# A graph attention layer: identity and root table first, sources turned in four pieces, half of the normalising on VectorE, small sums on POOL

## The chip, the cores and the metric

The kernel runs on one core of a Trainium2 chip. The core has five engines, each with its own in-order queue: TensorE (PE in the profile; PEld are its weight loads), VectorE (DVE), ScalarE (ACT), GpSimd (POOL) and SyncE (SP), which here only issues transfers. The engines wait for each other through semaphores alone. The metric is the device time of one execution in microseconds; the median of several runs counts.

## What is computed

Each of 12,500 nodes has a row x of 128 numbers; 212,500 edges, sorted by their target node, have attributes, a weight, a source and a target. The reference, cut to what matters:

```python
h = jnp.maximum(_layernorm(x, axis=-1), 0.0)
q = (h @ Wq.T + bq).reshape(N, NUM_HEADS, HEAD_DIM)          # 8 heads of 16
k = (edge_h @ Wk.T + bk).reshape(-1, NUM_HEADS, HEAD_DIM)
v = (h @ Wv.T + bv).reshape(N, NUM_HEADS, HEAD_DIM)
qs, qd = (q[src], q[dst])
in_m, out_m, diag_m = (qs * k).sum(-1), (qd * k).sum(-1), (qs * qd).sum(-1)
att = jnp.power(distance, lam)
score = (softmax(in_m * SCALE, dst) + softmax(out_m * SCALE, dst) + softmax(diag_m * SCALE, dst)) * att
agg = segment_sum(score[..., None] * v[dst], dst)
out = x + leaky_relu(agg.reshape(N, 128) @ Wo.T + bo, 0.1)
```

The three softmaxes run over the edges of one target node. The change touches only the first two lines and the preparation beside them: layer norm, ReLU, and the product with Wq.

## The kernel before

`ordered_path` does all the work for sorted targets. It has two parts.

**The preparation** (lines 690 to 982) fills two tables in DRAM: `q_table`, with one row of q for each node in float32, and `q3_table`, with the same row as three bfloat16 terms. The nodes lie in 98 tiles of 128 rows in one SBUF buffer `xq`, loaded in nine pieces by transfers on SP's queue. Four tiles make a group; there are 24 groups of four and one of two. The loop at line 925 runs over the groups g as a software pipeline. One turn of it issues, in this order:

- `rectify(g + 2)`, line 860: normalises and rectifies four tiles in place on ScalarE, one instruction for each tile, as ReLU(x * inv + shift), with inv and shift one number a row.
- `turn_h(g + 1)`, line 865: four transposes on TensorE through the identity matrix `ident` into one PSUM tile, then one ScalarE copy of 512 columns to `hT`.
- `nodes_q(g)`, line 873: four products with Wq into PSUM, one VectorE addition of the bias (line 880) back into `xq`, and the store of the group's rows to `q_table` on SP's queue (line 881).
- `ready(g + 4)` and `measure(...)`: the statistics, a few groups ahead. `statistics` (line 829) takes a loaded piece of 4, 4, 6 or 14 tiles: one bn_stats for each tile on VectorE, then five small VectorE operations on as many columns as there are tiles (lines 839 to 844), the "small sums". `scale` (line 847) makes inv and shift of them: a square root on ScalarE, a reciprocal and one more operation on VectorE.
- one entry of `side` (line 907), at the turns named there. `edges_0` lets POOL cast the source and target indices to float; `turn_ws` turns three weights; `biases` splits the biases in terms; `edges_1` turns the sources; `edges_2` turns the edge weights; `edges_3` makes thresholds and relative targets.

`turn_edges` (line 758) works on a quarter of the edges at a time: four transposes on TensorE into a PSUM tile `t_ps`, and one VectorE copy out of it (line 764). The pool of `t_ps` has two buffers, so the third quarter waits for the copy of the first. `edges_1` takes all four quarters at once. After it `step` may be written (line 782, POOL), since it lies where the sources lay.

After the loop POOL issues the first gathers (`gather`, line 645): indirect transfers of 128 rows of `q_table` each, which wait for all stores to that table. Then `terms_q` (line 887) makes and stores the three terms.

**The main loop** (line 1371) runs over 415 blocks of 512 edges. For each one POOL issues four gathers, twelve blocks ahead; TensorE turns and projects the edge attributes and spreads the targets' rows; VectorE multiplies and sums the logits; scans over the edges make the softmaxes' maxima.

What sets the order: `pin` (line 590) ties every instruction given to it behind the one pinned before it on the same engine. So the queues of the engines stand in the order in which the Python code runs. Instructions that aren't pinned, such as most constants at the top, are placed by the scheduler.

Of the kernel before, what the change touches and what calls it, by code (L numbers as in the profile page):

```python
# [7 lines left out]
F32 = mybir.dt.float32  # L8
BF = mybir.dt.bfloat16
I32 = mybir.dt.int32  # L10
AF = mybir.ActivationFunctionType
ALU = mybir.AluOpType
# [7 lines left out]
EPS = 1e-5  # L20
# [452 lines left out]
def ordered_path(ctx: ExitStack, tc: tile.TileContext, flag, x, src, dst, edge_attr, edge_weight,  # L473
# [19 lines left out]
    nc = tc.nc  # L493
    N, F = x.shape
    E = src.shape[0]
    P = 128
# [17 lines left out]
    NU, CU = NI // 2, 7  # L514
    CH = 2 * CU
# [6 lines left out]
    def parts_of(u):  # L522

        return [s for s in range(S)
                if (s == 0 or START * s - NEAR < UN * (u + 1))
                and (s == S - 1 or UN * u <= START * (s + 1) + NEAR)]
# [12 lines left out]
    sums = [dram.tile([NP, 2, 2 * H3], F32, name=f"sums{i}") for i in range(S)]  # L539


    consts = ctx.enter_context(tc.tile_pool(name="consts", bufs=1))
    jp = consts.tile([P, P], I32, name="jp")
    nc.gpsimd.iota(jp, pattern=[[1, P]], base=0, channel_multiplier=-1)
    ident = consts.tile([P, P], F32, name="ident")
    nc.vector.tensor_scalar(ident, jp, 0.0, None, op0=ALU.is_equal)

    third = consts.tile([P, 1], F32, name="third")
    threes = consts.tile([P, W], F32, name="threes")
    nc.gpsimd.iota(threes, pattern=[[3, W]], base=0, channel_multiplier=-1,  # L550
# [5 lines left out]
    ones3 = consts.tile([3, P], BF, name="ones3")  # L556
    nc.vector.memset(ones3, 1.0)

    eps = consts.tile([P, 1], F32, name="eps")
    nc.vector.memset(eps, EPS)  # L560
    wq, wv, wk, wo = [consts.tile([P, F], F32, name=n) for n in ("wq", "wv", "wk", "wo")]
    b3 = consts.tile([3, 3, F], BF, name="b3")
    bv3, bk3, bo3 = [b3[:, i, None, :].to_broadcast([3, JN, F]) for i in range(3)]
# [2 lines left out]
    inv = consts.tile([P, NI], F32, name="inv")  # L566
    shift = consts.tile([P, NI], F32, name="shift")
    blank = jp.bitcast(F32)[:, :2 * 2 * H3]
    nc.vector.memset(blank, 0.0)
    src_i = consts.tile([P, NB, JN], I32, name="src_i")  # L570
    att_t = consts.tile([P, NB, JN], F32, name="att_t")
# [12 lines left out]
    edges = ctx.enter_context(ExitStack())  # L584
    gath = edges.enter_context(tc.tile_pool(name="gath", bufs=QQ))
    load = edges.enter_context(tc.tile_pool(name="load", bufs=2))

    pinned = {}

    def pin(inst):  # L590

        engine = str(inst.ins.engine)
        if engine in pinned:
            tc.add_manual_dep(inst.ins, pinned[engine], mybir.DependencyInfo(
                mybir.DependencyClass.NoSync, mybir.DependencyReason.DATA), reason="in order")
        pinned[engine] = inst.ins.name
        return inst

    def rows_in(to, t, q):

        top, cut = (RW - 1) * RC, 96
        pin(q.dma_start(to[0:cut, :], t[:cut * RC].rearrange("(r c) -> r c", c=RC)))
        pin(q.dma_start(to[cut:RW - 1, :], t[cut * RC:top].rearrange("(r c) -> r c", c=RC)))
        pin(q.dma_start(to[RW - 1:RW, :E - top], t[None, top:E]))
# [85 lines left out]
    with tc.tile_pool(name="prep", bufs=1) as prep, \  # L690
# [10 lines left out]
        weight = prep.tile([RW, RC], F32, name="weight")  # L701
# [5 lines left out]
        xq = prep.tile([P, NI, F], F32, name="xq")  # L707
# [19 lines left out]
        for s in range(S):  # L727
            at = s * G * BE
            pin(nc.sync.dma_start(bases[:, :, s:s + 1], dst[None, at:at + G * BE + 1:BE, None]))
            n = min(T, (E - at - HEAD) // BE + 1)  # L730
            pin(nc.sync.dma_start(heads[:, :n, s:s + 1],
                                  dst[None, at + HEAD - 1:at + (n - 1) * BE + HEAD:BE, None]))
            n = min(T, (E - at) // BE)
# [24 lines left out]
        def turn_edges(of, to, which=range(RB)):  # L758
            cols = of.rearrange("r (a p j) -> r a j p", a=RB, j=JN)
            for a in which:  # L760
                t_ps = prep_ps.tile([P, JN, RW], F32, name="t_ps")
                for j in range(JN):
                    pin(nc.tensor.transpose(t_ps[:, j, :], cols[:, a, j, :], ident[:RW, :RW]))
                pin(nc.vector.tensor_copy(to[:, a:NB:RB, :], t_ps.rearrange("p j r -> p r j")))

        dst_f = dst_r.bitcast(F32)
        src_f = src_r.bitcast(F32)
# [6 lines left out]
        def edges_0():  # L774

            pin(nc.gpsimd.tensor_copy(src_f, src_r))
            pin(nc.gpsimd.tensor_copy(dst_f, dst_r))

        def edges_1():
            turn_edges(src_f, src_i)  # L780
            step = got["step"] = prep.tile([RW, RC + 1], F32, name="step", tag="step")
            pin(nc.gpsimd.tensor_sub(step, dst_f[:, 1:], dst_f[:, :RC + 1]))

        def edges_2():
            turn_edges(weight, att_t)

        def edges_3():
            of = got["cuts"] = of_tile()
# [20 lines left out]
        def turn_w(i, to):  # L809
            w_ps = prep_ps.tile([P, F], F32, name="t_ps")  # L810
            pin(nc.tensor.transpose(w_ps, w_in[:, i, :], ident))
            pin(nc.scalar.copy(to, w_ps))
# [16 lines left out]
        def statistics(lo, hi):  # L829

            n = hi - lo
            stats = node.tile([P, CH, 6], F32, name="stats", bufs=1)[:, :n]
            for i in range(n):
                pin(nc.vector.bn_stats(stats[:, i, :], xq[:, lo + i, :]))


            sums3 = node.tile([P, 3, CH], F32, name="sums3", bufs=4)[:, :, :n]
            total, apart, sq = sums3[:, 0], sums3[:, 1], sums3[:, 2]
            pin(nc.vector.tensor_add(total, stats[:, :, 1], stats[:, :, 4]))
            pin(nc.vector.tensor_sub(apart, stats[:, :, 1], stats[:, :, 4]))  # L840
            pin(nc.vector.tensor_add(sq, stats[:, :, 2], stats[:, :, 5]))
            pin(nc.vector.scalar_tensor_tensor(apart, apart, F / 4.0, apart, op0=ALU.mult,
                                               op1=ALU.mult))
            pin(nc.vector.tensor_add(sq, sq, apart))
            return lo, hi, total, sq

        def scale(lo, hi, total, sq):
# [9 lines left out]
        def tiles_of(g):  # L857
            return range(g * JN, min(NI, (g + 1) * JN))

        def rectify(g):  # L860
            for i in tiles_of(g):
                pin(nc.scalar.activation(xq[:, i, :], xq[:, i, :], AF.Relu, bias=shift[:, i:i + 1],
                                         scale=inv[:, i:i + 1]))

        def turn_h(g):
            n = len(tiles_of(g))
            h_ps = node_ps.tile([P, JN, P], F32, name="h_ps")
            for b, i in enumerate(tiles_of(g)):
                pin(nc.tensor.transpose(h_ps[:, b, :], xq[:, i, :], ident))
            hT = hTs[g] = node.tile([P, JN, P], F32, name="hT", bufs=2)  # L870
            pin(nc.scalar.copy(hT[:, :n], h_ps[:, :n]))

        def nodes_q(g):
            n = len(tiles_of(g))
# [12 lines left out]
        def terms_q(g):  # L887
# [8 lines left out]
            if g > 0:  # L896
# [7 lines left out]
                    q3_table[3 * lo:3 * (lo + n * P), :].rearrange("(u p k) f -> p u (k f)", p=P, k=6),  # L904
                    q3.rearrange("p (u k) t f -> p u (k t f)", k=2)))

        side = {0: edges_0, 4: turn_ws, 6: biases, 9: edges_1, 15: edges_2, 18: edges_3}
        turn_w(0, wq)
        parts = [(2 * lo, 2 * hi) for lo, hi in zip(LOADS, LOADS[1:])]

# [2 lines left out]
        def measure(upto):  # L913

            while parts and parts[0][0] < (upto + 1) * JN:
                measured.append(statistics(*parts.pop(0)))
# [8 lines left out]
        for g in range(-2, GN):  # L925
            if g + 2 < GN:
                rectify(g + 2)
            if 0 <= g + 1 < GN:
                turn_h(g + 1)
            if g >= 0:  # L930
                nodes_q(g)
            ready(g + 4)
            measure(g + 6 + min(max(g, 0), 6))
            if g in side:
                side[g]()
            if g == 9:
                fetch_edges(0)
                fetch_few()
# [161 lines left out]
    with tc.tile_pool(name="work", bufs=2) as work, \  # L1100
# [270 lines left out]
        for g in range(end):  # L1371
# [44 lines left out]
            if g < S:  # L1416
                of = [u for u in range(NU) if g in parts_of(u)]
# [56 lines left out]
@with_exitstack  # L1474
def kernel(ctx: ExitStack, tc: tile.TileContext, x, src, dst, edge_attr,
                              edge_weight, Wq, bq, Wk, bk, Wv, bv, Wo, bo, lam, out):

    nc = tc.nc  # L1480
    given = (x, src, dst, edge_attr, edge_weight, Wq, bq, Wk, bk, Wv, bv, Wo, bo, lam, out)
    flags = ctx.enter_context(tc.tile_pool(name="flags", bufs=1))
    flag = flags.tile([1, 1], I32, name="flag")
    ordered_path(tc, flag, *given)
    other = nc.values_load(flag[0:1, 0:1], min_val=0, max_val=1)
    with tc.If(other != 0):
        general_path(tc, *given)
# [29 lines left out]
```

## Time and profile before

| | |
|---|---|
| median of 7 runs | 2280.92 us (2274.59 to 2286.1) |
| the profiled execution, its own time | 2281.6 us |
| its span, first to last instruction | 2279.8 us |
| busy share of the span: PE, PEld, DVE, ACT, POOL | 74%, 59%, 87%, 59%, 73% |
| mean granted TensorE clock | 0.79 |
| first statistics on VectorE | at 4.33 us |
| first normalising on ScalarE | at 11.61 us |
| first store to q_table issued | at 50.64 us |
| last store to q_table issued | at 80.43 us |
| first gather | at 83.32 us |
| first block of the main loop on TensorE (L1133) | at 136.31 us |

The profile records one execution. Its rows name an instruction by its source line, its engine, and its output and inputs ("out<-in"). A number of instructions of one kind have a busy time, a mean duration and the idle time of the engine just before them, with what ended most of it. Two instructions of one engine can overlap by some 0.1 us, so start-to-start distances are used where a row of instructions is added up. All times are in microseconds from the start of the span, if nothing else is said.

### The profile page before, as it was taken

Reading aid. Unit: us, or ns where it says so; the run is one execution under the profiler, and the core shown is the slowest. Engines: PE = TensorE matmul, PEld = TensorE weight load, DVE = VectorE, ACT = ScalarE, POOL = GpSimd, SP = SyncE. Lnnn points to the kernel's source line nnn. Section 1 sums busy time; section 2 is a strip of 40 time slices with the busy share of each in tenths; the row PEclk is TensorE's granted clock in tenths of the full one; section 3 lists DMA queues with packets and bytes.
Section 4 is the critical chain, followed back from the end, with each engine's and each line's share of the span. In section 5 each row is a group of like instructions: output and inputs, shape, how many; then the busy total and the mean of one; then the engine's idle time right before and its main releaser. Section 6 shows DMA issues by size and latency. Waiting matters only on the chain.

```text
span 2279.8 us, 34664 instructions
## 1 busy us (share of the span) xinstructions
PE 1685.2 (74%) x10209; PEld 1341.1 (59%) x10209; DVE 1986.5 (87%) x2582; ACT 1346.3 (59%) x2445; POOL 1654.8 (73%) x1690
## 2 busy tenths in 40 slices
PE   5337887866767778877787778777786777777785
PEld 4335666655656556666565666656575666656564
DVE  7579999988989889898898998888898899889894
ACT  6646766655656556565565565555565565655571
POOL 3577777777777777777777777777777777777760
PEclk8768878877878887787778777777777887777777
DMA  6786455455445544455545554454545544555531
GB/s 196 246 269 184 146 162 168 139 158 150 138 146 149 164 141 141 145 167 149 147 141 168 152 147 137 144 171 141 148 132 163 161 143 140 145 166 150 151 100 56
DMA packets 314459, 351.19 MB, mean 154 GB/s; under 512 B 132882, under 2 KB 234013, under 8 KB 313952
## 3 DMA queue, kind: packets, MB, share of 16 engines
q1 hardware_dynamic: 245493, 233.57, 33.4%
q0 software_dynamic: 53344, 109.11, 17.3%
q10 hardware_dynamic: 15424, 6.19, 1.1%
q8 instruction: 83, 1.36, 0.2%
q14 instruction: 115, 0.94, 0.1%
HBM read 316.50 MB, written 32.17 MB: 153 GB/s over the span
## 4 chain that ended last, share of the span: by engine, by line
DMA 32%; PE 28%; DVE 18%; issue 12%; POOL 5%; ACT 5%; DVEq 0%; SPq 0%; ACTq 0%; POOLq 0%
DMA qq<-q_table,src_i 30%; PE k_ps L1125 10%; POOL qq L649 5%; PE w_ps L1272 5%; DVE prod L1145 4%; PE eT_ps L1116 4%; DVE prod L1146 3%; PE k_ps L1123 3%; DVE prod L1144 2%; PE qd_ps L1133 2%; PE node_ps L1056 2%; DMA q_table<-q 1%; DVE m L1212 1%; DVE back L1232 1%; PE d_ps L1258 1%
## 5 line engine op out<-in xcount | busy, mean ns | idle before, releaser
L649 POOL DMA_INDIRECT qq<-q_table,src_i x1660 | 1619.8, 976 | 512.8 <-issue 241.4
L1147 DVE TENSOR_REDUCE lT<-prod 128x96 f32<-128x1536 f32 x415 | 727.5, 1753 | 14.4
L1125 PEld LDWEIGHTS k_ps<-wk,eT 128*128 128x128 f32 x3320 | 514.6, 237 | 178.9 <-issue 69.3
L1125 PE MATMUL k_ps<-wk,eT 128*128 128x128 f32 x3320 | 608.7, 339 | 14.7 <-ACT eT L1118 14.3
L1133 PE MATMUL qd_ps<-win,oh 126*128 126x128 bf16 x1660 | 186.5, 244 | 422.6 <-DVE prod L1145 366.4
L1118 ACT COPY eT<-eT_ps 128x512 f32<-128x512 f32 x415 | 243.4, 587 | 356.9 <-PE eT_ps L1116 347.0
L1145 DVE TENSOR_TENSOR prod<-qq,qd_ps 128x512 f32<-128x512 f32 x415 | 283.2, 682 | 173.5 <-DMA qq<-q_table,src_i 172.3
L1133 PEld LDWEIGHTS <-oh 126*128 126x128 bf16 x1660 | 145.3, 109 | 483.1 <-issue 412.8
L1136 ACT COPY qd<-qd_ps 128x512 f32<-128x512 f32 x415 | 239.2, 576 | 144.7 <-PE qd_ps L1133 131.2
L1116 PE MATMUL eT_ps<-ident,ea 128*128 128x128 f32 x1660 | 316.8, 325 | 1.0 <-DVE found L954 1.0
L1110 ACT ACTIVATE relb<-relb,before 126x512 bf16<-126x512 bf16 x415 | 301.1, 726 | 0.0
L1144 DVE TENSOR_TENSOR prod<-qd,k_ps 128x512 f32<-128x512 f32 x415 | 279.3, 673 | 10.1 <-ACT qd L1136 5.7
L1146 DVE TENSOR_TENSOR prod<-qq,k_ps 128x512 f32<-128x512 f32 x415 | 282.6, 681 | 0.0
L1111 ACT ACTIVATE oh<-relb 126x512 bf16<-126x512 bf16 x415 | 261.4, 630 | 18.7 <-issue 5.5
L1116 PEld LDWEIGHTS eT_ps<-ident,ea 128*128 128x128 f32 x1660 | 253.8, 173 | 1.3 <-DVE found L954 1.3
L1272 PE MATMUL w_ps<-back,sel 128*126 128x144 f32 (+1 forms) x1344 | 209.7, 316 | 25.9 <-ACT sel L1262 21.1
L1272 PEld LDWEIGHTS w_ps<-back,sel 128*126 128x126 f32 (+1 forms) x1344 | 198.5, 215 | 35.4 <-ACT sel L1262 29.6
L1233 ACT ACTIVATE back<-back 128x480 f32<-128x480 f32 x83 | 50.1, 604 | 283.7 <-DVE back L1232 275.7
L1123 PE MATMUL k_ps<-b,ones 3*128 3x512 bf16 x415 | 184.3, 444 | 30.9 <-DVE prod L1146 28.9
L1200 DVE TENSOR_TENSOR_SCAN u<-far,u,l_ps 120x512 f32<-120x512 bf16 x82 | 104.4, 1273 | 9.6 <-PE l_ps L1167 6.9
L1212 DVE TENSOR_TENSOR_SCAN m<-far,head,u 120x512 f32<-120x512 bf16 x83 | 106.0, 1278 | 0.1
L1224 PE MATMUL m_ps<-ident,m 120*128 120x120 f32 x332 | 71.7, 355 | 40.2 <-DVE m L1212 39.1
(192 smaller groups left out, 1350.5 us busy)
## 6 DMA issues: line engine op xcount, KB each, us to landing
ea<-in_edge_attr_dram SPq DMA_DIRECT2D x83, 1280.0 KB
relb<-rel_d SPq DMA_DIRECT2D x83, 630.0 KB
qq<-q_table,src_i POOLq DMA_INDIRECT x1660
win<-q_table SPq DMA_DIRECT2D x415, 31.5 KB
far<-far_d SPq DMA_DIRECT2D x84, 120.2 KB
q_table<-q SPq DMA_DIRECT2D x24, 384.0 KB
sums<-rows SPq DMA_DIRECT2D x412, 7.9 KB
q_table<-xq SPq DMA_DIRECT2D x24, 256.0 KB
```

The lines of the kernel that those rows point to most:

```text
L649: rows = pin(nc.gpsimd.indirect_dma_start(out=qq[:, j, :], out_offset=None, in_=q_table, in_offset=bass.IndirectOffsetOnAxis(ap=src_i[:, g ...
L1110: pin(nc.scalar.activation(d, d, AF.Abs, bias=before[:K3]))
L1111: pin(nc.scalar.activation(oh, d, AF.Relu, bias=1.0, scale=-1.0))
L1116: pin(nc.tensor.transpose(eT_ps[:, j, :], eas[g // S][:, g % S, j * F:(j + 1) * F], ident))
L1123: pin(nc.tensor.matmul(k_ps, ones3, bk3, start=True, stop=False))
L1125: pin(nc.tensor.matmul(k_ps[:, j, :], eTs[g][:, j, :], wk, start=False, stop=(j == JN - 1)))
L1133: pin(nc.tensor.matmul(qd_ps[:, j, :], ohs[g][:, j * P:(j + 1) * P], d["win"][:, s, :], start=(j == 0), stop=(j == JN - 1)))
L1144: pin(nc.vector.tensor_mul(prod[:, :, 2, :], qds[g], ks[g]))
L1145: pin(nc.vector.tensor_mul(prod[:, :, 1, :], qqs[g], q_ps[g]))
L1146: pin(nc.vector.tensor_mul(prod[:, :, 0, :], qqs[g], ks[g]))
L1147: pin(nc.vector.tensor_reduce(lTs[t][:, :, s, :], prod.rearrange("p j i (h d) -> p j (i h) d", d=DIM), AX.X, ALU.add))
L1272: pin(nc.tensor.matmul(w_ps[:, i].rearrange("p s c -> p (s c)"), d["sel"][:n, j, lo:lo + 3, :].rearrange("p s w -> p (s w)"), d["back"][:n ...
```

## The change

- `pin` moves up, ahead of the constants. The identity, the constant `eps` and a new small tile `root` (a square root of `eps` on ScalarE) are pinned first.
- `edges_1` turns one quarter of the sources instead of four; three new steps `edges_1a`, `edges_1b`, `edges_1c` turn the others, one in a turn of the loop. The edge weights are turned in two steps of two quarters. The turns at which the steps run are moved.
- Of each group of four tiles, ScalarE normalises two (as Identity instead of ReLU) and VectorE two (multiply and add with the same columns inv and shift). The ReLU is now in ScalarE's copy out of the transposes' PSUM tile: a maximum with zero commutes with a transpose.
- The small sums of the six pieces of 14 tiles are made by POOL, those of the first three pieces still by VectorE. The one operation apart * F/4 * apart becomes a multiplication and a scaling. `stats` gets a second buffer.

The core of the diff:

```diff
     ident = consts.tile([P, P], F32, name="ident")
-    nc.vector.tensor_scalar(ident, jp, 0.0, None, op0=ALU.is_equal)
+    pin(nc.vector.tensor_scalar(ident, jp, 0.0, None, op0=ALU.is_equal))
+    eps = consts.tile([P, 1], F32, name="eps")
+    pin(nc.vector.memset(eps, EPS))
+    root = consts.tile([P, 1], F32, name="root")
+    pin(nc.scalar.activation(root, eps, AF.Sqrt))
...
+        def turn_src(a):
+            turn_edges(src_f, src_i, [a])
+
         def edges_1():
-            turn_edges(src_f, src_i)
+            turn_src(3)
             step = got["step"] = prep.tile([RW, RC + 1], F32, name="step", tag="step")
             pin(nc.gpsimd.tensor_sub(step, dst_f[:, 1:], dst_f[:, :RC + 1]))
+        def edges_1a():
+            turn_src(0)
...
         def edges_2():
-            turn_edges(weight, att_t)
+            turn_edges(weight, att_t, (0, 1))
+        def edges_2b():
+            turn_edges(weight, att_t, (2, 3))
...
-            stats = node.tile([P, CH, 6], F32, name="stats", bufs=1)[:, :n]
+            stats = node.tile([P, CH, 6], F32, name="stats", bufs=2)[:, :n]
...
-            sums3 = node.tile([P, 3, CH], F32, name="sums3", bufs=4)[:, :, :n]
-            total, apart, sq = sums3[:, 0], sums3[:, 1], sums3[:, 2]
-            pin(nc.vector.tensor_add(total, stats[:, :, 1], stats[:, :, 4]))
-            pin(nc.vector.tensor_sub(apart, stats[:, :, 1], stats[:, :, 4]))
-            pin(nc.vector.tensor_add(sq, stats[:, :, 2], stats[:, :, 5]))
-            pin(nc.vector.scalar_tensor_tensor(apart, apart, F / 4.0, apart, op0=ALU.mult,
-                                               op1=ALU.mult))
-            pin(nc.vector.tensor_add(sq, sq, apart))
+            sums2 = node.tile([P, 2, CH], F32, name="sums2", bufs=4)[:, :, :n]
+            total, sq = sums2[:, 0], sums2[:, 1]
+            apart = node.tile([P, CH], F32, name="apart", bufs=1)[:, :n]
+            of = nc.vector if lo < 2 * CU else nc.gpsimd
+            pin(of.tensor_add(total, stats[:, :, 1], stats[:, :, 4]))
+            pin(of.tensor_sub(apart, stats[:, :, 1], stats[:, :, 4]))
+            pin(of.tensor_add(sq, stats[:, :, 2], stats[:, :, 5]))
+            pin(of.tensor_mul(apart, apart, apart))
+            pin(of.tensor_scalar(apart, apart, F / 4.0, None, op0=ALU.mult))
+            pin(of.tensor_add(sq, sq, apart))
...
         def rectify(g):
             for i in tiles_of(g):
-                pin(nc.scalar.activation(xq[:, i, :], xq[:, i, :], AF.Relu, bias=shift[:, i:i + 1],
-                                         scale=inv[:, i:i + 1]))
+                if i % 4 < 2:
+                    pin(nc.scalar.activation(xq[:, i, :], xq[:, i, :], AF.Identity,
+                                             bias=shift[:, i:i + 1], scale=inv[:, i:i + 1]))
+                else:
+                    pin(nc.vector.tensor_scalar(xq[:, i, :], xq[:, i, :], inv[:, i:i + 1],
+                                                shift[:, i:i + 1], op0=ALU.mult, op1=ALU.add))
...
-            pin(nc.scalar.copy(hT[:, :n], h_ps[:, :n]))
+            pin(nc.scalar.activation(hT[:, :n], h_ps[:, :n], AF.Relu))
...
-        side = {0: edges_0, 4: turn_ws, 6: biases, 9: edges_1, 15: edges_2, 18: edges_3}
+        side = {4: turn_ws, 5: edges_0, 6: biases, 8: edges_1a, 9: edges_1b, 10: edges_1c, 11: edges_1,
+                13: edges_2, 14: edges_2b, 16: edges_3}
```

More of the change, by code (lines that the diff above doesn't have):

```diff
@@ L539, in ordered_path, with pin @@
     sums = [dram.tile([NP, 2, 2 * H3], F32, name=f"sums{i}") for i in range(S)]
+    pinned = {}
+    def pin(inst):
+        engine = str(inst.ins.engine)
+        if engine in pinned:
+            tc.add_manual_dep(inst.ins, pinned[engine], mybir.DependencyInfo(
+                mybir.DependencyClass.NoSync, mybir.DependencyReason.DATA), reason="in order")
+        pinned[engine] = inst.ins.name
+        return inst
     consts = ctx.enter_context(tc.tile_pool(name="consts", bufs=1))
@@ L557, in ordered_path @@
     nc.vector.memset(ones3, 1.0)
-    eps = consts.tile([P, 1], F32, name="eps")
-    nc.vector.memset(eps, EPS)
     wq, wv, wk, wo = [consts.tile([P, F], F32, name=n) for n in ("wq", "wv", "wk", "wo")]
@@ L586, in ordered_path @@
     load = edges.enter_context(tc.tile_pool(name="load", bufs=2))
[L588 to L597, printed above, removed]
     def rows_in(to, t, q):
@@ L777, in edges_0, with edges_1b, edges_1c @@
             pin(nc.gpsimd.tensor_copy(dst_f, dst_r))
+        def turn_src(a):
+            turn_edges(src_f, src_i, [a])
         def edges_1():
-            turn_edges(src_f, src_i)
+            turn_src(3)
             step = got["step"] = prep.tile([RW, RC + 1], F32, name="step", tag="step")
             pin(nc.gpsimd.tensor_sub(step, dst_f[:, 1:], dst_f[:, :RC + 1]))
+        def edges_1a():
+            turn_src(0)
+        def edges_1b():
+            turn_src(1)
+        def edges_1c():
+            turn_src(2)
         def edges_2():
-            turn_edges(weight, att_t)
+            turn_edges(weight, att_t, (0, 1))
+        def edges_2b():
+            turn_edges(weight, att_t, (2, 3))
         def edges_3():
```

## The prediction

> **What bounds the kernel now.** I read the page first, then the chain of waits, then the table of windows, then the timeline of the first 90 us. The chain says where a saved microsecond counts. These are its pieces between 46 and 86 us (start, length, what), from the chain in order of time:
>
> ```profile
> 46.51 1.94 DVE stats L834 x10
> 49.17 0.51 DVE src_i L764
> 49.73 1.66 PE t_ps L763 x8
> ...
> 55.25 1.65 ACT xq L862 x4
> 56.90 0.47 ACT hT L871
> 57.36 1.55 ACT xq L862 x4
> 58.91 0.45 ACT hT L871
> ...
> 79.86 0.41 DVE xq L880
> 80.26 0.61 DVE xq L895
> ```
>
> So the making of q lies on the path from its first load to the last add at 80.26. First VectorE holds it (statistics), then ScalarE: four normalisings and a copy, the groups starting 2.02 us apart (55.25, 57.27). The windows show a hole between the two (window, length, PE, PEld, DVE, ACT, POOL, clock, DMA share, GB/s):
>
> ```profile
> 30.00:40.00 10.00, 8.14 (x45) 6.45 (x44) 9.86 (x37) 8.91 (x23) 2.22 (x2) 0.83 0.49 117
> 40.00:50.00 10.00, 1.99 (x18) 1.82 (x17) 9.76 (x38) 3.14 (x8) 1.57 (x1) 0.71 0.06 1
> 50.00:60.00 10.00, 9.78 (x65) 9.13 (x65) 4.86 (x11) 7.56 (x20) 8.35 (x2) 0.77 0.75 245
> ```
>
> TensorE works 2 of 10 us there, while VectorE is full: the third piece of the turned sources needs a PSUM buffer that only the VectorE copy L764 frees, and that copy stands at 49.09, behind a backlog. Afterwards VectorE is half idle. What follows: the gathers start when the last q store has landed, and they pace the rest (group, busy, mean, idle before):
>
> ```profile
> L649 POOL DMA_INDIRECT qq<-q_table,src_i x1660 | 1619.8, 976 | 512.8 <-issue 241.4
> ```
>
> The first gather stands at 83.32, and from 300 to 2200 us VectorE waits 172.3 us for gathered rows. From the stage that writes q3_table on, the built program has the same instructions in the same order on every engine, so I carry an earlier end of q over one for one: gain = 83.3 minus the new start of the gathers.
>
> **The change part by part.**
>
> *Start.* ident moves from 8.41 on VectorE to its head, and the square root's table (one ACT_TABLE_LOAD, 1.28 at 9.57) replaces the copy's table load at 0.74. The first normalising stands at 11.61. Now the statistics of the second load end at 8.49 as before, plus 0.2 for one more small operation; square root 0.3, reciprocal and shift 0.4: some 9.4, 2.2 earlier. Lower bound 0: ident and threes now meet POOL's three memsets of 1.8 us (1.28 to 6.57), and if each waits for one, the statistics start up to 2.2 late.
>
> *VectorE's load.* From the first statistics at 4.33 to 80.26 are 75.9 us. Idle in them (groups by shape): 13.4 before L880, 1.1 before L834, 2.3 before L850, 1.3 before L754, 1.0 before L764: 19.1, so 56.8 of work. Added: 48 normalisings of 128x128. No such row exists. Below: L834 reads the same tile at 0.20 each (14 in 2.79). Above: L794, the same operation on 512 columns, starts 0.40 apart. I take 0.20, since the columns are those of L834: 9.6 (to 19.2). A multiplication in three small sums: 0.6. Removed: six small sums of 14 tiles, 0.61 each (29.24 to 29.85): 3.7. Sum 56.8 + 9.6 + 0.6 - 3.7 = 63.3.
>
> *POOL's side of the sums.* Six operations of 14 columns; the smallest POOL rows are 0.10 (a memset) and 0.19 (L550), so 0.6 to 1.2 a set, and with a handover between dependent ones I allow 1.5. Five of six are covered by the backlog of VectorE (two sets of statistics between a set and its use). The first isn't: its reciprocal stands next in VectorE's queue, with two normalisings and an add behind it: 1 to 2 us late, inside the 2.2 won at the start.
>
> *The lock between VectorE and POOL.* This is the dear term. Timeline lines (start, length):
>
> ```profile
> 34.20 1.89 POOL L776 CAST src_r<-src_r 104x2048 f32<-104x2048 int32 x1 [13.88 <-DMA b_row<-in_L_gnn_bv_dram]
> 34.24 1.89 DVE L839 TENSOR_TENSOR sums<-stats 128x14 f32<-128x14 f32 x1
> 39.67 1.90 POOL L777 CAST dst_r<-dst_r 104x2050 f32<-104x2050 int32 x1 [3.58 <-DMA dst_r<-in_dst_dram]
> 40.94 0.67 DVE L839 TENSOR_TENSOR sums<-stats 128x14 f32<-128x14 f32 x1
> ```
>
> An addition that takes 0.18 elsewhere ends each time with POOL's cast. It already costs 1.7 + 0.5 here. Adds from PSUM and statistics run beside POOL. Does a normalising stop? L794 passes 512 columns in 0.40, more than one a cycle of the 0.20 row, and ident (L546, 0.31) ended at 8.72 just after POOL's iota at 8.64: I take yes.
>
> The Trainium skill, "SBUF — State Buffer", section "Who interferes with whom", says that a tensor_scalar in its two-port mode and any POOL instruction exclude each other for the whole instruction; by it the blocks below are paid and my sum stands; without it only two-input additions stop and the end is that of the first rival. No row here shows the new instruction beside POOL.
>
> With one normalising pair per group the block nearly always hits. Casts of 1.9 at 34.2 and 39.7: 1.3 and 1.7, of which 2.2 were paid before. step (L782, 3.61) starts when the sources are turned, near 51.3: 3.4. rel (L797, 3.92) starts right behind L794, with a normalising next: 3.9 less the 1.3 that TensorE still has in hand, 2.6. L789 (7.12) hides a library reload, since a two-input L851 at 59.90 ran 0.17 inside it; in the changed program the reload ahead of it is gone. I price it 0, at worst 7.
>
> *Sources in four pieces.* Same four copies (0.5 each on VectorE), same transposes, each beside a group. The hole of 8 us closes, but VectorE's backlog, which made it, stays.
>
> *Two of four on VectorE, ReLU in the copy.* ScalarE's group falls from 2.02 by two of 0.41 to 1.20; the copy with ReLU becomes 0.63 instead of 0.57 (bf16 rows L1111 against L871): 1.26. TensorE's group takes 1.33 (54.56 to 55.89); I take 1.42.
>
> **The sum.** Up to the last statistics (48.44 before): minus 3.1 (five sums), 2.2 (old blocks), 4.5 (idle before 25 us), plus 4.4 (22 normalisings), 1.1 (small operation, first piece), 3.0 (blocks), 1.4 (waits for square roots): about 48.5. The next two groups with three pieces and the block of 3.4: the add of the thirteenth group near 55.5 (56.99 before). Twelve groups at 1.42 are 17.0 (23.3 before, 56.99 to 80.26); turned weights 1.5 and rel 2.6 on top: 76.6. About a microsecond of blocks should fall into slack: 75.7, 4.6 earlier. The stores then also are close to their own limit: 7552 KB (24 x 256, 128 and ea's 1280), 7.73 MB, all behind the loads on SP's queue, whose first store stays at 50.64. At 343 to 379 GB/s (windows 52:54 and 68:70, DMA share over 1) that is 20.4 to 22.5 us from 51.6: landed at 72.0 to 74.1, not before. So 4.6 stands: profiled execution 2281.6 (span 2279.8) - 4.6 = 2277.0; the median of the runs is 2280.92, 0.7 lower: 2276.3.
>
> **The rivals.**
>
> *Stores decide.* If the blocks cost little (a normalising slips between POOL's instructions, or isn't stopped), take 3.0, 3.4 and 2.6 away: compute ends at 67 to 70, and the gathers start when the stores have landed, 73 to 75. Gain 8.3 to 10.3: 2271.5. For it: DMA share 0.18 to 0.5 between 72 and 80 is free. Against: four rows above.
>
> *Hidden anyway.* The q3 stage moves 9.6 MB at some 250 GB/s beside the gathers; if it were bound by bytes alone from 80 us on, an earlier start would be given back there. For it: ScalarE waits 21.2 us in that stage for stores to land (L894). Against: the DMA share is 0.77 between 80 and 136, and these stores stand behind q's on SP's queue, so their backlog moves with them. 2280.
>
> *VectorE becomes the bound (slower).* One mechanism: the normalisings and their locks. At 0.40 a piece (9.6 more) and every POOL instruction paid in full (1.9 + 1.9 + 3.6 + 7.1 + 3.9 = 18.4): 4.3 + 1.2 of waits + 63.3 - 2.2 of old blocks + 9.6 + 18.4 = 94.6, 14.3 later than 80.3: 2295. It decides against the change once that excess of the pieces and the locks together pass 80.3 - 66.6 = 13.7. For it: VectorE is full from 30 to 50 already. Against: half of its later time is free, so part of every block is made up.
>
> **How the numbers follow.** A measurement of this kernel tells 0.3%, 6.8 us, from no change. Forecast (gain 2 to 7.5) 0.48; stores decide 0.33; hidden 0.10; slower 0.09, of which 0.07 beyond 0.3%. Faster by over 0.3%: the stores' case 0.33 and the forecast's upper end 0.09, so 0.42. Within 0.3%: the rest of the forecast 0.39, hidden 0.10, 0.02 of the last, 0.51. Range: from 2270 (stores' best case, 10.3) to 2284, past the hidden case by a part of VectorE's bounds; the forecast's own is 2273 to 2279.
>
> **What would show it.** Right: TensorE's busy time in 40 to 50 us above 6; ScalarE's groups 1.3 to 1.5 apart after 56; normalisings on VectorE of 2 to 3 us that end with POOL's step and rel; first gather at 78 to 79.5. Stores' case: no such long normalisings, last add before 72, DMA share near 1 until 73. Slower: normalisings 0.40 apart, last add after 80. I am wrong at the root if the gathers start earlier and the end doesn't follow.

## The result and the profile after

| | before | after |
|---|---|---|
| median | 2278.09 us (46 runs) | 2291.17 us (18 runs) |
| ratio, 95% interval | | 1.0053 [1.0044, 1.0063] |
| the profiled execution, its span | 2281.6, 2279.8 us | 2291.57, 2289.8 us |
| mean granted TensorE clock | 0.79 | 0.80 |
| first normalising | at 11.61 us | at 9.41 us |
| last statistics end | at 48.44 us | at 52.63 us |
| first gather | at 83.32 us | at 96.19 us |
| first block of the main loop on TensorE | at 136.31 us | at 147.40 us |
| last gather | at 2210.26 us | at 2217.96 us |

The kernel became slower by 13.1 us between the medians, 0.53% by the ratio. The making of q ends 12.9 us later, and the gathers start that much later. The table of windows of the changed kernel (window, length, PE, PEld, DVE, ACT, POOL, clock, DMA share, GB/s):

```profile
30.00:40.00 10.00, 6.55 (x51) 5.61 (x51) 9.53 (x37) 6.13 (x16) 5.08 (x14) 1.00 0.48 114
40.00:50.00 10.00, 6.61 (x34) 6.49 (x35) 7.16 (x22) 2.72 (x6) 3.38 (x7) 0.66 0.07 2
50.00:60.00 10.00, 5.80 (x46) 4.87 (x44) 9.96 (x27) 4.30 (x10) 5.84 (x8) 0.99 0.80 259
60.00:70.00 10.00, 3.59 (x19) 3.59 (x20) 7.88 (x8) 1.56 (x4) 6.27 (x1) 0.50 0.67 216
```

The hole at 40 to 50 us is closed (TensorE 6.61 instead of 1.99). A new one stands at 60 to 70: TensorE 3.59, ScalarE 1.56, while POOL is in one instruction and VectorE seems busy with eight. What they are, the timeline shows (start, length, engine, line, what; in brackets how long the engine was idle before it and what ended that):

```profile
55.46 3.60 POOL L787 TENSOR_TENSOR step<-dst_r 104x2049 f32<-104x2049 f32 x1 [1.13 <-PE t_ps L765]
...
56.61 9.74 DVE L885 TENSOR_SCALAR xq<-xq,inv,shift 128x128 f32<-128x128 f32 x2
...
59.15 7.12 POOL L806 TENSOR_SCALAR of<-step 104x2048 bf16<-104x2048 f32 x1
...
63.68 2.67 DVE L903 TENSOR_TENSOR xq<-q_ps,bq_all 128x512 f32<-128x512 f32 x1
...
66.98 0.60 ACT L894 ACTIVATE hT<-h_ps 128x512 f32<-128x512 f32 x1 [9.55 <-PE h_ps L892]
...
77.61 4.13 DVE L885 TENSOR_SCALAR xq<-xq,inv,shift 128x128 f32<-128x128 f32 x2
...
77.77 3.88 POOL L814 CAST of<-dst_r 104x2048 bf16<-104x2048 f32 x1 [11.50 <-DVE dst_r L811]
```

Two normalisings that take 0.6 us elsewhere take 9.74, from inside POOL's step to the end of POOL's thresholding (66.27), and ScalarE waits 9.55 us for the transposes behind them. A second pair, at 77.61, ends with POOL's rel (81.65). These normalisings share no tile with the POOL instructions beside them, and their rows name nothing that they wait for: the profile books the time as VectorE's work. So the engines here wait for each other not through semaphores alone, as the introduction has it; VectorE is also held while POOL runs, which is called a lock below. The view of the one line (duration in ns: least, median, greatest) says how rare this is: the normalisings are not slow in general, a few of the 48 are.

```profile
L885 DVE TENSOR_SCALAR xq<-xq,inv,shift x48: 325/340/7289, 9.7 to 89.2; 128x128 f32<-128x128 f32 x48
```

The chain of waits of the changed kernel (start, length, what) shows what comes after such a block:

```profile
77.69 4.06 DVE xq L885 x2
81.75 0.04 issue
81.79 0.47 PE h_ps L892
82.27 1.71 PE q_ps L900 x8
...
87.36 0.89 PE q_ps L900 x8
```

A product of four tiles takes 1.71 us just after the block and 0.89 five microseconds later. In windows of some 2 us the granted clock is 0.50 from 81.7 to 86 us and 1.00 from 88 to 90; after the first block it is 0.50 from 66 to 70 and 0.97 from 70 to 72. So after each of the two blocks TensorE works at half its clock for some 4 us, and the path pays that too. From the gathers on little differs (group, busy, mean, idle before):

```profile
L651 POOL DMA_INDIRECT qq<-q_table,src_i x1660 | 1614.6, 973 | 520.2 <-issue 248.4
```

1614.6 us of gathers against 1619.8, 520.2 of idle against 512.8.

### The profile page after: what moved, and what is told of

Read it like the earlier page. It is cut to its first block, busy times and chain, and to the rows that moved or that the text cites. A ratio compares the mean times of both kernels' runs of the same rounds, so it can differ in the third digit from the quotient of the medians.

```text
span 2289.8 us, 34688 instructions
## 1 busy us (share of the span) xinstructions
PE 1673.9 (73%) x10209; PEld 1336.2 (58%) x10209; DVE 2007.5 (88%) x2603; ACT 1329.2 (58%) x2397; POOL 1659.3 (72%) x1726
## 3 DMA queue, kind: packets, MB, share of 16 engines
q0 software_dynamic: 53344, 109.11, 17.4%
## 4 chain that ended last, share of the span: by engine, by line
PE 30%; DMA 26%; DVE 18%; issue 12%; POOL 6%; ACT 4%; SPq 0%; DVEq 0%; POOLq 0%; ACTq 0%
DMA qq<-q_table,src_i 26%; PE k_ps L1149 10%; POOL qq L651 6%; PE w_ps L1296 5%; DVE prod L1169 5%; PE eT_ps L1140 4%; DVE prod L1170 3%; PE k_ps L1147 3%; DVE prod L1168 3%; PE qd_ps L1157 2%; PE node_ps L1080 1%; DVE u L1224 1%; DVE m L1236 1%; DVE back L1256 1%; DVE lT L1171 1%
## 5 line engine op out<-in xcount | busy, mean ns | idle before, releaser
L651 POOL DMA_INDIRECT qq<-q_table,src_i x1660 | 1614.6, 973 | 520.2 <-issue 248.4
```

Source lines behind the costliest of these rows:

```text
L651: rows = pin(nc.gpsimd.indirect_dma_start(out=qq[:, j, :], out_offset=None, in_=q_table, in_offset=bass.IndirectOffsetOnAxis(ap=src_i[:, g ...
```

## The experiments

Two theories stood against each other. *Locks:* a normalising on VectorE can't run beside a long POOL instruction, and these waits cost the 13 us. *Load:* VectorE had no room for 48 normalisings, locks or not. And a third question: why don't the other parts of the change, which the windows show to work, bring anything?

Some of the experiments ran on chips on which the main loop is slower and the kernel before takes 2668 or 2696 us; so each is compared with the kernel before on its own chip, and where in the preparation the gathers start is read from its profile.

### The parts apart

**All normalisings on ScalarE** (the rest of the change stays):

```diff
-                if i % 4 < 2:
-                    pin(nc.scalar.activation(xq[:, i, :], xq[:, i, :], AF.Identity,
-                                             bias=shift[:, i:i + 1], scale=inv[:, i:i + 1]))
-                else:
-                    pin(nc.vector.tensor_scalar(xq[:, i, :], xq[:, i, :], inv[:, i:i + 1],
-                                                shift[:, i:i + 1], op0=ALU.mult, op1=ALU.add))
+                pin(nc.scalar.activation(xq[:, i, :], xq[:, i, :], AF.Identity,
+                                         bias=shift[:, i:i + 1], scale=inv[:, i:i + 1]))
```

> All four tiles of a group are normalised by ScalarE again; everything else of the change stays. Lock theory (POOL's long step, thresholding and cast stop VectorE's normalisings, and that is the whole loss): no normalising on VectorE, ScalarE's 25 groups at 2.03 us from 9.4 us with 3 to 6 us of waits, last add at 66 to 72 us, first gather at 74 to 77 instead of 83.3 in the kernel before and 96.2 in the changed one, time 6 to 9 us under the kernel before. Rival 'another part of the change costs' (POOL's sums, identity first, pieces): first gather still past 88, time 5 us or more over the kernel before.

2669.14 us, ratio 1.0003 [0.9993, 1.0014], first gather at 83.57. So without the split of the normalisings the loss is gone; but the rest gains nothing, against 6 to 9 us expected. The timeline of this kernel offers a reason, which a later run tests:

```profile
53.35 7.12 POOL L806 TENSOR_SCALAR of<-step 104x2048 bf16<-104x2048 f32 x1
...
54.04 3.86 DVE L870 SCALAR_TENSOR_TENSOR shift<-sums,inv 128x14 f32<-128x14 f32 x1
...
66.72 3.84 POOL L814 CAST of<-dst_r 104x2048 bf16<-104x2048 f32 x1 [6.26 <-DVE dst_r L811]
...
67.43 3.17 DVE L870 SCALAR_TENSOR_TENSOR shift<-sums,inv 128x14 f32<-128x14 f32 x1
```

The shift, fourteen columns that take 0.17 us elsewhere, takes 3.86 and 3.17 here, and all normalisings wait for it. The first ends 4.55 us after the start of the thresholding, 2.57 before that ends; the second ends with rel.

**The split alone**, on the kernel before:

```diff
             for i in tiles_of(g):
-                pin(nc.scalar.activation(..., AF.Relu, ...))
+                if i % 4 < 2:
+                    pin(nc.scalar.activation(..., AF.Identity, ...))
+                else:
+                    pin(nc.vector.tensor_scalar(..., op0=ALU.mult, op1=ALU.add))
...
-            pin(nc.scalar.copy(hT[:, :n], h_ps[:, :n]))
+            pin(nc.scalar.activation(hT[:, :n], h_ps[:, :n], AF.Relu))
```

> The kernel before with one part of the change alone: two tiles of four normalised by VectorE and ReLU in the copy. Lock theory: step, thresholding and cast of POOL stop a normalising each for 3, 7 and 3.9 us, VectorE's backlog up to 48 us grows by some 5 us more; first gather at 92 to 98, time 8 to 15 us over the kernel before. Rival 'another part costs': first gather within 3 us of 83.3, time equal.

2691.4 us, 1.0087 [1.0073, 1.0102], 23.4 us slower, first gather at 105.40: more than expected. The last statistics end at 58.89 there (48.44 before), and a shift of fourteen columns takes 3.61 beside the thresholding. Without the rest of the change (the pieces, POOL's small sums, the early start, the moved turns) the split loses some 10 us more, so that rest does carry something in the changed kernel.

**The normalising with two inputs** (the column shift as a second, broadcast tensor):

```diff
-                    pin(nc.vector.tensor_scalar(xq[:, i, :], xq[:, i, :], inv[:, i:i + 1],
-                                                shift[:, i:i + 1], op0=ALU.mult, op1=ALU.add))
+                    pin(nc.vector.scalar_tensor_tensor(xq[:, i, :], xq[:, i, :], inv[:, i:i + 1],
+                        shift[:, i:i + 1].to_broadcast([P, F]), op0=ALU.mult, op1=ALU.add))
```

> The changed kernel with VectorE's normalising written as an instruction with two SBUF inputs (shift spread over the columns as the second input), so that it runs at one column a cycle. Lock theory: it is no longer stopped by the thresholding of 7.12 us (a two-input instruction of 14 columns ran 0.17 us inside it in the kernel before) but still by step and by the casts; longest normalising under 4.5 us, first gather at 87 to 90, time 5 to 9 us under the changed kernel. Rival 'VectorE has too much work': 48 instructions of about the same length, first gather at 96, time equal to the changed kernel.

2673.6 us, 1.0029 [1.0018, 1.004], 5.6 us slower, first gather at 90.27. Elsewhere a pair takes 0.60 us, as in the other form. It still waits, but less; the longest normalising is 4.69 us, where under 4.5 was expected:

```profile
54.44 3.62 POOL L787 TENSOR_TENSOR step<-dst_r 104x2049 f32<-104x2049 f32 x1 [1.12 <-PE t_ps L765]
...
55.61 7.21 DVE L885 SCALAR_TENSOR_TENSOR xq<-xq,inv,shift 128x128 f32<-128x128 f32 x2
...
58.14 7.12 POOL L806 TENSOR_SCALAR of<-step 104x2048 bf16<-104x2048 f32 x1
```

The pair ends at 62.82, 4.68 us into the thresholding, much as the first shift did (4.55) with all normalisings on ScalarE; the form with one input was held until 7.20 us after its start.

**The long edge work on VectorE** (step, thresholding, rel), so that nothing long is left on POOL after the casts:

```diff
-            pin(nc.gpsimd.tensor_sub(step, dst_f[:, 1:], dst_f[:, :RC + 1]))
+            pin(nc.vector.tensor_sub(step, dst_f[:, 1:], dst_f[:, :RC + 1]))
...
-            pin(nc.gpsimd.tensor_scalar(of, got["step"][:, :RC], 0.0, -FAR, ...))
+            pin(nc.vector.tensor_scalar(of, got["step"][:, :RC], 0.0, -FAR, ...))
...
-            pin(nc.gpsimd.tensor_copy(rel_b.rearrange(...), ...))
+            pin(nc.vector.tensor_copy(rel_b.rearrange(...), ...))
```

> The changed kernel with step, thresholds and the cast of the relative targets made by VectorE instead of POOL. Lock theory: nothing of POOL longer than 1.9 us is left beside the groups, no normalising over 2.1 us; VectorE gets some 5.5 us of work more, but loses 13 us of blocks; first gather at 85 to 89, time 6 to 10 us under the changed kernel. Rival 'VectorE has too much work': 5 us more work, first gather at 100, time 4 to 6 us over the changed kernel.

2671.6 us, 1.0014 [1.0003, 1.0025], 3.6 us slower, first gather at 89.63. No normalising takes over 0.42 us, and the first gather still stands 6.3 us behind that of the kernel before. So there is a load beside the locks: VectorE, with 5.5 us more of edge work and 48 normalisings, is still behind.

### Locks or load

**The changed kernel again**, unedited, beside the next three:

> The changed kernel itself, beside the next three on one chip. If the 12.9 us by which its first gather starts later are what it loses, then the first gather stands at 96 to 97 us here too (83.3 in the kernel before), and the time is 12 to 14 us above the kernel before, whatever this chip's gathers cost afterwards. If part of the loss lay in the main loop, the difference would grow or shrink with the chip.

2291.9 us against 2278.28, 1.0056 [1.0037, 1.0076]; first gather at 95.82. As expected.

**POOL's three long instructions in four pieces each**, with normalisings as in the changed kernel (the thresholding is shown; step and rel are cut likewise):

```diff
-            pin(nc.gpsimd.tensor_scalar(of, got["step"][:, :RC], 0.0, -FAR, ...))
+            for lo in range(0, RC, 512):
+                pin(nc.gpsimd.tensor_scalar(of[:, lo:lo + 512], got["step"][:, lo:lo + 512], 0.0, -FAR, ...))
```

> The changed kernel with POOL's three long instructions (step, thresholding, rel) each issued as four of a quarter of the columns. If VectorE's normalisings wait for the end of one POOL instruction and then get in, the longest normalising falls from 7.29 to about 1.8 us (7.12 / 4), the first gather from 96.2 to 79 to 82, and the time is 1 to 5 us below the kernel before. If POOL's next piece takes the lock again before VectorE gets in, the longest normalising stays above 5 us, the first gather stays past 92, and the time stays 9 us or more above the kernel before.

2280.43 us, 1.0015 [1.0, 1.003]; first gather at 85.37. The greatest normalising is 1.18 us instead of 7.29:

```profile
55.94 1.95 DVE L890 TENSOR_SCALAR xq<-xq,inv,shift 128x128 f32<-128x128 f32 x2
...
58.41 1.18 DVE L890 TENSOR_SCALAR xq<-xq,inv,shift 128x128 f32<-128x128 f32 x2
...
58.90 7.97 POOL L808 TENSOR_SCALAR of<-step 104x512 bf16<-104x512 f32 x4
```

VectorE gets in between the pieces. Cutting POOL's instructions, which takes no work away and adds 0.85 us to the thresholding, gives back 10.4 of the 12.5 us by which the gathers started later. It didn't reach the 79 to 82 us that I expected if only locks were left out: the last statistics still end at 51.95 us, near the changed kernel's 52.63 and not as before, and the four subtractions, now beside the pieces of rel, take 3.51 us instead of 1.68. So the locks are most of the loss; that the rest is VectorE's load fits these rows, but no run shows it apart.

**Normalisings on VectorE only from group 12 on**, when the statistics are done, and the edge work on VectorE:

```diff
-                if i % 4 < 2:
+                if i % 4 < 2 or g < 12:
```

> Normalisings on ScalarE alone up to group 11, while VectorE is full of statistics, two of four on VectorE from group 12 on; step, thresholding and rel on VectorE, so that POOL holds nothing long after the casts. If the loss is the locks and VectorE's load before 53 us, and the split itself is worth what was forecast (groups 1.33 to 1.42 us apart), the last add stands near 74, the first gather at 75 to 77, and the time is 6 to 8 us below the kernel before. If the split is no gain even without locks (VectorE the bound, or the stores), the first gather is at 82 or later and the time within 2 us of the kernel before.

2278.47 us, 1.0009 [0.9998, 1.0021]; first gather at 81.77. A miss: 5 us later than expected. The thresholding, subtractions and rel stand in one block on VectorE's queue (62.73 to 67.73), and ScalarE waits 4.61 us behind it.

**All normalisings on ScalarE and the edge work on VectorE:**

> All normalisings on ScalarE, as in e1_all_scalar, and step, thresholding and rel on VectorE. In e1 the first gather stood at 83.57 although the start was 2.2 us earlier, and two shifts of 14 columns took 3.86 and 3.17 us beside POOL. If these locks ate the gain, the shifts take 0.17 here, the first gather stands at 78 to 81 and the time is 2 to 5 us below the kernel before. If ScalarE's groups of 2.02 us or the clock of TensorE ate it, the first gather stays at 83 and the time is that of the kernel before.

2273.95 us, 0.9982 [0.997, 0.9994]; first gather at 79.88. This is the first version below the kernel before. The shifts take 0.17 us. One wait of ScalarE for a shift is left after 50 us:

```profile
60.75 1.22 DVE L806 TENSOR_SCALAR of<-step 104x2048 bf16<-104x2048 f32 x1
...
62.08 1.68 DVE L811 TENSOR_SCALAR dst_r<-dst_r,base_c 104x512 f32<-104x512 f32 x4
...
63.79 2.03 DVE L814 CAST of<-dst_r 104x2048 bf16<-104x2048 f32 x1
...
66.67 0.17 DVE L870 SCALAR_TENSOR_TENSOR shift<-sums,inv 128x14 f32<-128x14 f32 x1
...
66.88 1.65 ACT L882 ACTIVATE xq<-xq,shift,inv 128x128 f32<-128x128 f32 x4 [2.20 <-DVE shift L870]
```

Thresholding takes 1.22 us on VectorE and 7.12 on POOL, so moving it there costs less than its lock.

### What is left, and what the start is worth

**The block on VectorE in three turns instead of one**, once on the version with ScalarE alone and once on the late split:

```diff
-                13: edges_2, 14: edges_2b, 16: edges_3}
+                13: edges_2, 14: edges_2b, 16: edges_3, 18: edges_3b,
+                20: edges_3c}
```

> As e8_scalar_no_locks, with the thresholding, the four subtractions and rel on VectorE in three turns (16, 18, 20) instead of one. In e8 they stood together from 60.75 to 65.74 us, and the shift behind them made ScalarE wait 2.20 us. If that wait is on the path, the first gather comes 1.5 to 2.5 us before e8's 79.88 and the time falls to 6 us below the kernel before. If TensorE's or ScalarE's own groups bound it, it stays within 0.7 us of 79.88.

2692.06 us against 2696.39, 0.9984 [0.9974, 0.9995]; first gather at 76.91, 3.0 us before that of the version in one block (79.88), more than the 1.5 to 2.5 expected. The time didn't follow: 4.3 us below the kernel before, as with one block, where 6 were expected; the interval, 1.3 to 7.0, doesn't tell the two apart. The stores to q_table now fill the transfers to the end (windows, same columns as above):

```profile
70.00:72.00 2.00, 1.85 (x15) 1.58 (x14) 1.23 (x3) 1.78 (x5) 0.00 (x0) 1.00 1.09 384
72.00:74.00 2.00, 1.17 (x11) 0.97 (x9) 1.44 (x4) 1.13 (x3) 0.00 (x0) 1.00 1.07 377
74.00:76.00 2.00, 0.00 (x0) 0.00 (x0) 1.92 (x4) 1.52 (x3) 0.00 (x0) 1.00 0.85 274
```

> As e7_late_split, spread in the same way. In e7 ScalarE waited 4.61 us behind the one block on VectorE. If that wait is on the path, the first gather comes from 81.77 to 77 to 78.5 us, and the time is 3 to 5 us below the kernel before. If VectorE's work in all (normalisings and the edge work on the same engine) bounds it, the first gather stays past 80.5.

2693.52 us, 0.9989 [0.998, 0.9997]; first gather at 80.18. That is 1.6 us earlier where 3.3 or more were expected, and it stays behind the version with ScalarE alone. VectorE is what remains: it is busy for 9.60 of the 10 us from 60 to 70, with the thresholding, the subtractions and a pair of normalisings in every group, and ScalarE waits 0.7 to 2.5 us before most groups (copies at 55.35, 57.62, 59.89, 69.60, 74.10). So this split is no gain over ScalarE alone even without locks.

**The kernel before with its edge work on VectorE**, nothing else:

> The kernel before with step, thresholding and rel on VectorE and nothing else changed. In it none of the three met a waiting shift (the shift at 59.90 ran in 0.17), so by the lock theory nothing is won: the first gather stands at 83 to 86 us (VectorE has 5.5 us more to do) and the time is 0 to 3 us above the kernel before. If moving the three is itself what made e8 fast, the first gather comes at 80 here too.

2695.4 us, 0.999 [0.9979, 1.0002]; first gather at 82.85. Moving the three alone wins nothing that can be told. They had harmed no shift before: the one that fell into the thresholding came late in it (see below).

**Identity and root table as before**, on the version with ScalarE alone and no locks:

> As e8_scalar_no_locks, with ident, eps and the square root's table as in the kernel before, so that the first normalising stands at 11.6 instead of 9.4 us. If the 2.2 us of the start reach the end, the first gather stands at 82 us and the time is about 2 us above e8's. If VectorE's backlog up to 50 us takes them back, the first gather stays at 79.9 to 80.4.

2693.58 us, 0.9989 [0.998, 0.9999]; first gather at 78.84:

```profile
11.90 2.42 ACT L881 ACTIVATE xq<-xq,shift,inv 128x128 f32<-128x128 f32 x6 [0.25 <-DVE shift L869]
```

The first normalising is 2.5 us later than in the version with the early start (9.4), and the gathers don't start later (78.84 against 79.88, on another chip; why they start even earlier than expected stays open). No worth of the early start can be told. What gives that version its 3.4 us is, by what is left, the pieces, POOL's small sums and the moved turns, once the locks are out of their way; these weren't tried apart.

### One number decides

First gather minus 83.32 (the kernel before, profiled on the first chip only), beside the difference of the medians to the kernel before on the same chip, in us:

| kernel | first gather | time |
|---|---|---|
| the changed kernel | +12.9 | +13.1 |
| all on ScalarE | +0.3 | +1.2 |
| the split alone | +22.1 | +23.4 |
| two inputs | +7.0 | +5.6 |
| edge work on VectorE | +6.3 | +3.6 |
| the changed kernel again | +12.5 | +13.6 |
| cut in four | +2.1 | +2.2 |
| late split | -1.6 | +0.2 |
| ScalarE alone, no locks | -3.4 | -4.3 |
| the same, spread | -6.4 | -4.3 |
| late split, spread | -3.1 | -2.9 |
| before, edge work on VectorE | -0.5 | -1.0 |
| ScalarE alone, no locks, late start | -4.5 | -2.8 |

The two columns agree within 2.7 us over a range of 28.5, though the main loops of these chips differ by some 400 us. Among the kernels that start earlier the agreement is no finer than the noise: 3.4 and 6.4 us of earlier start both come with 4.3 us of time.

## Why the prediction was wrong

The forecast was 2276.3 us with a range from 2270 to 2284; 2291.17 was measured, and the rival with VectorE as the bound, at 2295 us, is the nearest. Along the path the kernel was behind the forecast by 4.1 us at the last statistics (52.63 against 48.5), by 10.2 at the end of the thirteenth group's add (66.35 against 55.5 and the add's own 0.69) and by 17.4 at the end of the adds (93.1 against 75.7). By the forecast's own steps:

**What bounds, and that the end of q carries over one for one: right.** The table above shows it for later starts, over 20 us. The "hidden anyway" rival spoke of earlier ones; there the table gives 1.0 to 4.3 us for 0.5 to 6.4, apart from one kernel at -1.6 and +0.2, so most of it is ruled out, but not to the microsecond.

**Start: right in place, wrong in worth.** The first normalising stands at 9.41, as forecast, though ident and the first small sum's scaling met POOL's memsets (0.72 and 0.94 us). But the 2.2 us were carried on as "4.5 idle before 25 us". VectorE's idle time from the first to the last statistics (all gaps between its timeline rows, added up) is 6.3 us in both kernels. Up to 25 us it fell from 5.8 to 3.0, not by 4.5; and as much returns later (0.5 before, 3.3 now), most of it as waits for TensorE and ScalarE at 45.92 and 49.23 (1.22 and 1.51). The late start showed the same from the other side.

**VectorE's load: too small by the piece.** I took 0.20 us a normalising, from the statistics' rate. Pairs stand 0.51 apart, 0.26 each. Up to the last statistics there are 24 of them, some 6.2 us instead of 4.4. With the idle time that stayed, less the casts' locks, which were smaller than forecast (one shift of 0.75), the last statistics end at 52.63 instead of 48.5.

**The lock: the step that failed.** I priced step 3.4, rel 2.6 and the thresholding **0**, "since a two-input L851 at 59.90 ran 0.17 inside it", with a library reload as the explanation of POOL's 7.12 us. The two rows of the kernel before behind this reading:

```profile
55.26 7.12 POOL L789 TENSOR_SCALAR of<-step 104x2048 bf16<-104x2048 f32 x1
...
59.90 0.17 DVE L851 SCALAR_TENSOR_TENSOR shift<-sums,inv 128x14 f32<-128x14 f32 x1
```

Measured, less 0.34 each: step 2.1 (2.45), rel 3.5 (3.87), and the thresholding 7.0 (7.29). Both reasons fell. By the prediction's own words the reload is gone from the changed program, and the instruction still takes 7.12; cut in four, each piece takes 1.92 to 1.95 us, the first no longer than the others, so no one-off reload hides in it and the time is its own. And the row that I read as "not locked" began 4.64 us after POOL's start (59.90 less 55.26), while the two-input operations that were held ended 4.55 and 4.68 us after it in the runs above. It had come late enough, nothing more. It was also of another kind than the instruction that was to be priced, which is held for all 7.2. I had a bound of 7 for this term and took its other end on one row, whose offset inside the POOL instruction I didn't look at. This term is the largest single error of the sum, 7.0 us; step came 1.3 smaller and rel 0.9 larger than priced.

The Trainium skill, "SBUF — State Buffer", section "Who interferes with whom", has both kinds: an operation with two SBUF inputs against a GpSimd instruction that reads SBUF, and a tensor_scalar in its two-port mode against any. For the second this trace agrees (7.29 us, to the end; that the normalising is in that mode is not shown, the form with two inputs takes the same 0.60 a pair), and the prediction misread the page: by it the thresholding had to be paid too, so the sum with 0 for it did not follow. For the first it agrees that there is a lock, but the page (in "SBUF: two separate sides") has it last for the whole instruction, and here it ended after some 4.6 of 7.12.

**What the blocks cost beyond themselves: not in the sum.** I let "about a microsecond of blocks fall into slack". Instead the last twelve groups lost 7.2 us against the forecast (17.4 less 10.2), of which rel's excess is 0.9. After a block the group restarts from an empty pipeline, ScalarE waiting for TensorE and VectorE for both, at half the clock (1.71 instead of 0.89 us for a product). The twelve groups at 1.42 us are right where nothing blocks: ScalarE's copies stand 1.33 apart at 72.92, 74.25 and 75.58. But the distances between the copies at 66.98, 70.65 and 72.92, and at 75.58, 82.36, 84.92 and 87.46, are 2.3 to 6.8; the first two of them hold the turned weights too.

**The stores' rival: its floor was not put to the test.** Stores were to land at 72.0 to 74.1 at best. In the fastest preparation found the transfers are full until 74 and the first gather stands at 76.91, but there the last add ends only at 73.85, so the stores alone did not hold it. The changed kernel, with a DMA share of 0.67 at 60 to 70, never came near it.

**The slower rival: right in mechanism, and its size by luck.** It forecast the end of the adds at 94.6; they end at 93.1. I gave it 0.09. Its condition, 13.7 us of excess and locks together, was met by three POOL instructions (12.6) and the pieces' excess (2.9). But it had summed 28.0 for the two where 15.5 were measured, and 1.2 for VectorE's waits where all gaps of VectorE from the first statistics to the end of the adds come to 13.0: two errors of some 12 us that cancel.

## What to carry to other kernels

Before an elementwise step is moved to VectorE, lay every long POOL instruction of that stretch over its queue: the price can be the rest of that instruction, plus a restart of what waits at half the clock, and a short operation that passed unharmed only says something if it began early in the POOL instruction. A POOL instruction that does one simple pass over 2000 columns is worth comparing with VectorE's own time (7.12 against 1.22 us here), or cutting into pieces (12.5 us of delay became 2.1). And a part that speeds up one engine can shift another into a lock: here the other parts of the change gained nothing while the shifts were held, and 4.3 us when they weren't (0.9982 [0.997, 0.9994]).

## What the runs showed of the hardware that was not expected

- The lock's length depends on VectorE's operation: beside POOL's thresholding (7.12 us, float32 to bfloat16) held two-input operations ended 4.55 to 4.68 us after its start, tensor_scalar from SBUF to SBUF 7.20. In the changed kernel the addition queued behind the held normalising is recorded from 63.68 on, 4.53 us after the thresholding's start, too; what POOL gives up at that point no run shows. Additions out of PSUM and the reciprocal ran beside the thresholding at their usual 0.69 and 0.24, a copy out of PSUM beside step at 0.58.
- POOL takes 3.5 ns a column for that thresholding, 1.8 for a subtraction of two float32 tensors (3.60 for 2049), 0.9 for an int32 cast (1.89 for 2048). VectorE takes 0.6, 1.1 and, for rel's permuted cast that costs POOL 3.88, 1.0.
- POOL's memsets and iota, which read nothing, hold up a tensor_scalar of 4 or 6 columns too: 0.45 to 1.10 us in the three small sums at the start, against 0.14 for one of a single column at 4.63, beside a memset.
